# Attention scores in PSUM banks chosen by an account of expected times, and the narrower kind of scores first

## The chip, the cores and the metric

The kernel runs on one core of a Trainium2 chip. Its engines work from queues of their own: TensorE (PE in the profile, and PEld for its weight loads) multiplies matrices into PSUM; VectorE (DVE) and ScalarE (ACT) read PSUM; GpSimd (POOL) works in SBUF; SyncE (SP) issues most DMAs. A wait in a queue holds everything behind it in that queue. The metric is the device time of one execution in microseconds; the median of several runs counts.

## The reference, cut to what matters

Two layers over x of shape (2, 1024, 128), all in fp32: a retention block with group norm, latent attention (16 heads of 8, causal) with an expert choice behind it, plain attention (16 heads of 8) and a ternary-weight product, each followed by a residual sum and a layer norm. The change touches the two softmax attentions alone:

```
scores = jnp.einsum('bhqd,bhkd->bhqk', q, k) / np.sqrt(HEAD_DIM)     # first attention
causal = jnp.tril(jnp.ones((t, t), dtype=bool))
scores = jnp.where(causal, scores, -jnp.inf)
attn = jax.nn.softmax(scores, axis=-1)
out = jnp.einsum('bhqk,bhkd->bhqd', attn, v)
...
weights = jax.nn.softmax(scores, axis=-1)                            # second, not causal
out = jnp.einsum('bhqk,bhkd->bhqd', weights, v)
```

## The kernel before

The retention block takes the first 260 us. Then one long hand-ordered stretch (`tc.manual_schedule()`) runs both attentions as a chain of 224 items in ticks, with the other work of the layers (`side_work`: projections, experts, layer norms, outputs) put between the ticks. The order of instructions on every engine is the order of the Python calls.

**Steps and items.** A step is one attention (`a` = 0 causal, 1 plain), sequence `b`, block `k` of 512 queries and group `g` of four heads. The four heads of a group lie in the four row groups of 32 partitions, so that products of different heads can run in TensorE at once. Each step has *score items* (`s_items`: 128 queries against up to 512 keys) and, in the same number, *exponential items* (`t_items`: 128 keys against up to 512 queries). In the plain attention all of them have 512 columns; in the causal one they have 128, 256, 384 or 512.

**A tick** (`chain_tick`, L456) does, for the score item of this tick and the exponential item of 11 ticks earlier (`AHEAD`):
- first half: products `sc` of heads 0 and 1 (`score`), products `sct` of heads 2 and 3 (`shifted`), then DVE's row maxima of the two sc (`maxima`, L348 with the causal mask, L353 without) and ACT's exponentials of the two sct (`exps`, L397);
- second half: the same with heads 2 and 3 for sc, 0 and 1 for sct;
- where the causal diagonal needs it, a select on POOL (`bar`, L405);
- `product`: the exponentials of the item before, all four heads, times the values into one bank `acc`, which ACT copies out (L419, L422) and POOL adds up (L423);
- once a step: DVE joins the maxima (`shifts`), PE transposes them (`m_ps`, `enter`), and SP writes them into a row of q, so that sct comes out already lowered by the maximum; `finish` transposes the sums (`o_ps`) and DVE divides.

So a full tick writes nine PSUM tiles of one bank each: eight scores and acc. Side work takes more: `ph` and `pmoe` (the experts' products), `xn_ps`, `lpr`, `loT_ps` and others.

**Banks.** PSUM has eight banks in this kernel's pools. In this stretch every tile comes from `slot(name)`, which hands out the banks in a ring. A tile's first product waits until the last reader of the bank's previous tile is done; nothing else ties a bank to its user. In a full tick the ninth tile, acc, therefore gets the bank of the same tick's first sc, and every score tile gets a bank of the tick before.

Of the kernel before, what the change touches and what calls it, by code (L numbers as in the profile page):

```python
# [8 lines left out]
F32 = mybir.dt.float32  # L9
# [5 lines left out]
P = 128  # L15
B, T = 2, 1024
BT = 512
# [3 lines left out]
NG, GH, HD = 4, 4, 8  # L21
HW = 32
# [5 lines left out]
VW = HD + 1  # L28
VN = (NH - 1) * VW + HW
AHEAD = 11  # L30
# [30 lines left out]
def block_kernel(  # L61
# [19 lines left out]
    def mm(o, lhsT, rhs, start=True, stop=True):  # L81
        nc.tensor.matmul(o, lhsT, rhs, start=start, stop=stop)  # L82
# [64 lines left out]
    v_aug = [early.tile([P, T // P, VN], F32, name="v_aug_0")]  # L147
# [8 lines left out]
    banks, scratch_of = [None], [None]  # L156

    def slot(name):
        return banks[0](name)

    def ring_of(pools):
        turn = [0]

        def bank(name):

            at = turn[0] % 8
            turn[0] += 1
            return pools[at // 6].tile([P, BT], F32, tag=f"b{at}", name=name)

        return bank  # L170

    def hrows(j):
        return slice(j * HW, (j + 1) * HW)
# [140 lines left out]
    s_items, t_items = [], []  # L314
# [7 lines left out]
            t_items += [(i, kt, 0) for kt in range(T // P)]  # L322
    s_last = {it[0]: n for n, it in enumerate(s_items)}
    t_last = {it[0]: n for n, it in enumerate(t_items)}
    parts, lowered, es, sums, pools, o_tok = {}, {}, {}, {}, {}, []

    def score(item, heads):
        i, c, half, n = item
        a, b, k, g = steps[i]
        tok = slice(k * BT + c * P, k * BT + (c + 1) * P)  # L330
        if i not in parts:
            parts[i] = small.tile([P, NC, GH, NB], F32, tag="parts", name="parts")
        got = []
        for j in heads:
            sc = slot("sc")
            rws = hrows(j)
            mm(sc[:, :n], qT[b][rws, g, tok], kT[b][rws, g, half * BT : half * BT + n])
            got.append((j, sc))
        return got

    def maxima(item, got):
        i, c, half, n = item
        a, b, k, g = steps[i]
        for j, sc in got:
            part = parts[i][:, c, j, half : half + 1]
            if a == 0 and half == k:
                spare = early.tile([P, BT], F32, tag="spare", name="spare")
                nc.vector.tensor_tensor_reduce(  # L348
                    out=spare[:, :n], in0=sc[:, :n], in1=causal[:, BT - n :], scale=1.0,
                    scalar=-3.0e38, op0=ALU.add, op1=ALU.max, accum_out=part,  # L350
                )
            else:
                nc.vector.tensor_reduce(part, sc[:, :n], AX.X, ALU.max)  # L353

    def shifts(i):

        a, b, k, g = steps[i]
        n_half = NB if a else k + 1
        lowered[i] = small.tile([P, GH, NC], F32, tag="lowered", name="lowered")
        nc.vector.tensor_reduce(  # L360
            lowered[i].rearrange("p j c -> p c j"), parts[i][:, :, :, :n_half], AX.X, ALU.max,
            negate=True,
        )

    def enter(i):

        a, b, k, g = steps[i]
        tp = slot("m_ps")
        nc.tensor.transpose(
            tp[: GH * NC, :P], lowered[i].rearrange("p j c -> p (j c)"), ident  # L370
        )
        rows_of = small.tile([GH * NC, P], F32, tag="m_rows", name="m_rows", bufs=2)
        nc.scalar.copy(rows_of, tp[: GH * NC, :P])
        nc.sync.dma_start(out=qT[b][ONE::HW, g, block_of(k)], in_=rows_of)

    def shifted(n_item, heads):
        i, kt, lo = t_items[n_item]
        a, b, k, g = steps[i]
        n = BT - lo
        if n_item not in es:  # L380
            es[n_item] = pools["work"].tile([P, GH, BT], F32, tag="es", name="es")
        got = []
        for j in heads:
            sct = slot("sct")
            rws = hrows(j)
            mm(
                sct[:, :n], kT[b][rws, g, kt * P : (kt + 1) * P],
                qT[b][rws, g, k * BT + lo : (k + 1) * BT],
            )
            got.append((j, sct))  # L390
        return got

    def exps(n_item, got):
        i, kt, lo = t_items[n_item]
        n = BT - lo
        for j, sct in got:
            nc.scalar.activation(es[n_item][:, j, :n], sct[:, :n], AF.Exp, scale=scale)  # L397

    def bar(n_item):

        i, kt, lo = t_items[n_item]
        a, b, k, g = steps[i]
        if a == 0 and kt * P >= k * BT:
            d = es[n_item][:, :, :P]
            nc.gpsimd.affine_select(  # L405
                out=d, in_=d, pattern=[[0, GH], [1, P]], compare_op=ALU.is_ge, fill=0.0,
                base=0, channel_multiplier=-1,
            )

    def product(n_item):  # L410
        i, kt, lo = t_items[n_item]
        a, b, k, g = steps[i]
        acc = slot("acc")
        for j in range(GH):
            at = (g * GH + j) * VW
            mm(acc[hrows(j), lo:], v_aug[b][:, kt, at : at + HW], es[n_item][:, j, : BT - lo])
        if kt == 0:
            sums[i] = pools["work"].tile([P, BT], F32, tag="oT", name="oT")
            nc.scalar.copy(sums[i], acc)  # L419
        else:  # L420
            part = pools["work"].tile([P, BT], F32, tag="part", name="part", bufs=1)
            nc.scalar.copy(part[:, lo:], acc[:, lo:])  # L422
            nc.gpsimd.tensor_tensor(sums[i][:, lo:], sums[i][:, lo:], part[:, lo:], ALU.add)  # L423

    def finish(i):
        a, b, k, g = steps[i]
        tp = transposed(sums[i].rearrange("p (c t) -> p c t", c=NC), "o_ps")
        tp = tp.rearrange("p (h w) -> p h w", w=HW)
        rec = small.tile([P, NC * GH], F32, tag="rec", name="rec")
        nc.vector.reciprocal(rec, tp[:, :, ONE])  # L430
        nc.vector.tensor_tensor(
            o_tok[b][k][:, :, g * GH * HD : (g + 1) * GH * HD].rearrange(
                "p c (j d) -> p c j d", d=HD
            ),
            tp[:, :, :HD].rearrange("p (c j) d -> p c j d", c=NC),
            rec.rearrange("p (c j) -> p c j", c=NC).unsqueeze(3).to_broadcast([P, NC, GH, HD]),
            ALU.mult,
        )

    n_items = len(s_items)  # L440
# [15 lines left out]
    def chain_tick(tick):  # L456
        si = tick if tick < n_items else None
        ti = tick - AHEAD if 0 <= tick - AHEAD < n_items else None
        for s_heads, t_heads in (((0, 1), (2, 3)), ((2, 3), (0, 1))):
            got_s = score(s_items[si], s_heads) if si is not None else ()  # L460
            got_t = shifted(ti, t_heads) if ti is not None else ()
            if si is not None:
                maxima(s_items[si], got_s)
            if ti is not None:
                exps(ti, got_t)
        if ti is not None:
            bar(ti)
        if si is not None and s_last[s_items[si][0]] == si:
            shifts(s_items[si][0])
        ai = tick - AHEAD - 1  # L470
        if 0 <= ai < n_items:
            product(ai)
        si = tick - 1
        if 0 <= si < n_items and s_last[s_items[si][0]] == si:
            enter(s_items[si][0])
        ai = tick - AHEAD - 3
        if 0 <= ai < n_items and t_last[t_items[ai][0]] == ai:
            finish(t_items[ai][0])


    with ExitStack() as rc:
# [29 lines left out]
        at, n = R_CONST["cs"]  # L511
# [307 lines left out]
        with tc.manual_schedule():  # L819
# [46 lines left out]
            n = n_chunks - 1  # L866
# [11 lines left out]
        ring = []  # L878
        rp.close()
        ring.append(ctx.enter_context(  # L880
            tc.tile_pool(name="ring", bufs=1, space=PSUM, reuse_waits="tile")
        ))
        banks[0] = ring_of(ring)
        with tc.manual_schedule():
            chain_tick(0)
            normal(n, r)
            rs.close()
            ring.append(ctx.enter_context(tc.tile_pool(
                name="ring2", bufs=1, space=PSUM, side="right", reuse_waits="tile"
            )))  # L890
            aside(n, 1)
            chain_tick(1)
            pt, og = gated(n)
            affine(n, pt, og, range(RH))
            chain_tick(2)
            nc.vector.tensor_tensor(og, og, sg[n], ALU.mult)
            block = output(n, og)
            chain_tick(3)
            layer_norm(*block)
# [5 lines left out]
    for i, name in enumerate(("w1", "w2")):  # L905
        at, n = M_W[name]
# [179 lines left out]
    class Job:  # L1086
        def __init__(self, at, by, stages, after=()):
            self.at, self.by, self.stages, self.after, self.done = at, by, stages, after, False
# [177 lines left out]
```

## Time and profile before

| what | us |
|---|---|
| median of three runs | 1195.03 |
| lowest and highest | 1191.51, 1197.48 |
| the profiled execution, its time | 1191.54 |
| the profiled execution, its span | 1189.8 |
| mean granted TensorE clock in it | 0.975 |

The views are read as follows. A timeline line gives the start in us, the time in us to the end of a run of equal instructions, engine, source line, operation, out<-in, its shape and the number of instructions; in brackets the idle time before it and what ended that. A line L82 is the helper `mm` that records most products, so products are told apart by their tiles. An fp32 product stands as two matmul records, and a tick's length is read from the first `sc` of one tick to the first `sc` of the next.

Ticks begin at 264 us with tick 4. In the windows of the stretch, PE is busy 424.7 of the 452 us from 264 to 716 (the causal attention with most of the side work), 102.8 of the 104 us to 820 and 296.5 of the 316 us to 1136 (nearly all of the plain attention); DVE 313.4, 72.6 and 259.7; ACT 251.3, 65.2 and 239.5.

### The profile page before, as it was taken

The page shows a single profiled execution, that of the slowest core. Times are in us where ns is not written, and L with a number is a line of the kernel's source. Part 1 is how long each engine was busy: PE and PEld are TensorE (multiplying, and loading weights), DVE is VectorE, ACT ScalarE, POOL GpSimd, SP SyncE. Part 2 cuts the span into 40 slices and gives each one's busy share as a digit, 9 for nine tenths or more (in the row PEclk, how much of TensorE's full clock was granted, in tenths as well). Part 3 has the DMA queues.
Part 4 walks back from the last instruction along what each step waited for, and adds up shares of the span by engine and source line. Part 5 has one row for each costly group of instructions (what it writes and reads, how often), then busy time and mean ns, then how long its engine had stood idle before and what let it go on. Part 6 is the DMA issues. An engine that isn't in the chain of part 4 may idle for free.

```text
span 1189.8 us, 22189 instructions
## 1 busy us (share of the span) xinstructions
PE 1102.6 (93%) x8554; PEld 604.3 (51%) x8554; DVE 825.9 (69%) x1822; ACT 710.4 (60%) x1439; POOL 479.8 (40%) x491
## 2 busy tenths in 40 slices
PE   6999999979889999999999999999989989998993
PEld 5888888755444554554444444444333333333322
DVE  4666766757766667676666677667788888888812
ACT  2465544432666556655565557556768867886891
POOL 4466445411656434443353334423333333323342
PEclk9999999986999999999999999999999999999996
DMA  5511112101000000100010001000100000000000
GB/s 187 164 37 45 41 41 45 28 10 73 10 11 19 1 2 1 21 3 1 2 19 1 1 4 18 2 1 1 19 10 2 1 2 10 1 2 10 1 1 9
DMA packets 14840, 25.56 MB, mean 21 GB/s; under 512 B 2960, under 2 KB 8400, under 8 KB 14352
## 3 DMA queue, kind: packets, MB, share of 16 engines
q1 hardware_dynamic: 14080, 22.30, 7.7%
q8 instruction: 67, 1.10, 0.4%
q0 software_dynamic: 224, 1.05, 0.2%
q10 hardware_dynamic: 432, 0.81, 0.2%
q14 instruction: 37, 0.30, 0.1%
HBM read 10.13 MB, written 1.05 MB: 9 GB/s over the span
## 4 chain that ended last, share of the span: by engine, by line
PE 72%; DVE 17%; POOL 4%; issue 3%; ACT 2%; DMA 1%; SPq 0%; POOLq 0%; DVEq 0%; ACTq 0%
PE sc L82 17%; PE acc L82 15%; PE sct L82 12%; PE pmoe L82 5%; PE ph L82 5%; DVE parts L353 5%; DVE spare L348 2%; PE py L82 2%; PE pv L82 2%; PE pr L82 2%; PE pout L714 1%; PE o_ps L187 1%; PE pg L82 1%; DVE x L205 1%; ACT es L397 1%
## 5 line engine op out<-in xcount | busy, mean ns | idle before, releaser
L397 ACT ACTIVATE es<-sct 128x512 f32<-128x512 f32 (+3 forms) x896 | 426.9, 558 | 218.6 <-PE sct L82 169.0
L353 DVE TENSOR_REDUCE parts<-sc 128x1 f32<-128x512 f32 x640 | 396.9, 682 | 94.4 <-PE sct L82 69.0
L82 PE MATMUL sc<-kT,qT 32*128 32x512 f32 (+3 forms) x1792 | 428.4, 584 | 5.5 <-DVE parts L348 2.7
L82 PE MATMUL sct<-qT,kT 32*128 32x512 f32 (+3 forms) x1792 | 410.6, 578 | 1.4 <-DMA qT<-m_rows 1.1
L423 POOL TENSOR_TENSOR oT<-oT,part 128x512 f32<-128x512 f32 (+3 forms) x192 | 217.5, 1133 | 392.3 <-ACT part L422 388.0
L82 PE MATMUL acc<-es,v_aug 128*32 128x512 f32 (+3 forms) x1792 | 221.6, 558 | 40.6 <-DVE parts L353 29.0
L82 PEld LDWEIGHTS sc<-kT,qT 32*128 32x128 f32 x1792 | 171.7, 189 | 145.2 <-DVE parts L353 73.9
L82 PEld LDWEIGHTS sct<-qT,kT 32*128 32x128 f32 x1792 | 179.1, 184 | 46.0 <-issue 23.3
L348 DVE CUSTOM_DVE_ANT_0 spare<-sc,causal 128x512 f32<-128x512 f32 (+3 forms) x256 | 125.4, 490 | 48.2 <-PE sc L82 12.8
L82 PEld LDWEIGHTS acc<-es,v_aug 128*32 128x32 f32 x1792 | 37.8, 108 | 196.0 <-DVE parts L353 112.5
L422 ACT COPY part<-acc 128x512 f32<-128x512 f32 (+3 forms) x192 | 105.7, 550 | 42.4 <-PE acc L82 36.3
L405 POOL TENSOR_SCALAR_AFFINE_SELECT es<-es 128x512 f32<-128x512 f32 x64 | 40.8, 637 | 118.5 <-ACT es L397 118.5
L771 ACT ACTIVATE og<-pt,cols_sb 128x128 f32<-128x128 f32 x128 | 46.5, 468 | 53.1 <-PE pt L763 53.1
L82 PEld LDWEIGHTS pmoe<-m_w,hT 128*128 128x128 f32 x512 | 59.6, 192 | 16.2 <-DVE parts L353 8.8
L82 PE MATMUL pmoe<-m_w,hT 128*128 128x128 f32 x512 | 65.0, 280 | 0.6 <-DVE parts L348 0.2
L82 PE MATMUL ph<-xnT,m_w 128*128 128x512 f32 x128 | 62.4, 610 | 0.0
L118 POOL TENSOR_TENSOR rstd<-rstd,nhalf 128x4 f32<-128x4 f32 (+1 forms) x44 | 54.7, 1244 | 3.6
L970 DVE TENSOR_SCALAR hT<-ph,cols_sb 128x512 f32<-128x512 f32 x32 | 24.0, 750 | 35.2 <-PE ph L82 35.2
L645 POOL TENSOR_TENSOR swap<-swap,r_cs 128x1024 f32<-128x1024 f32 x16 | 38.7, 2417 | 20.7 <-DMA swap<-plain 20.7
L982 DVE SCALAR_TENSOR_TENSOR moe_acc<-pmoe,oh,moe_acc 128x128 f32<-128x128 f32 x64 | 22.4, 350 | 35.2 <-PE pmoe L82 34.8
L668 ACT COPY v<-pv 128x1024 f32<-128x1024 f32 x16 | 16.2, 1012 | 43.8 <-PE pv L82 43.8
L82 PEld LDWEIGHTS ph<-xnT,m_w 128*128 128x128 f32 x128 | 21.7, 189 | 31.0 <-issue 11.0
(178 smaller groups left out, 1190.1 us busy)
## 6 DMA issues: line engine op xcount, KB each, us to landing
swap<-plain SPq DMA_DIRECT2D x64, 128.0 KB
qT<-dense SPq DMA_DIRECT2D x32, 64.0 KB
kT<-dense SPq DMA_DIRECT2D x32, 64.0 KB
m_w<-in_m_w SPq DMA_DIRECT2D x2, 1024.0 KB
x<-in_x SPq DMA_DIRECT2D x4, 256.0 KB
mcs<-in_m_const SPq DMA_DIRECT2D x4, 256.0 KB
out<-ob SPq DMA_DIRECT2D x4, 256.0 KB
r_rest<-in_r_const POOLq DMA_DIRECT2D x1, 774.0 KB, 7.4
```

The lines of the kernel that those rows point to most:

```text
L82: nc.tensor.matmul(o, lhsT, rhs, start=start, stop=stop)
L118: nc.gpsimd.tensor_tensor(r, r, nhalf[:, :n], ALU.pow)
L348: nc.vector.tensor_tensor_reduce(out=spare[:, :n], in0=sc[:, :n], in1=causal[:, BT - n :], scale=1.0, scalar=-3.0e38, op0=ALU.add, op1=ALU ...
L353: nc.vector.tensor_reduce(part, sc[:, :n], AX.X, ALU.max)
L397: nc.scalar.activation(es[n_item][:, j, :n], sct[:, :n], AF.Exp, scale=scale)
L405: nc.gpsimd.affine_select(out=d, in_=d, pattern=[[0, GH], [1, P]], compare_op=ALU.is_ge, fill=0.0, base=0, channel_multiplier=-1,)
L422: nc.scalar.copy(part[:, lo:], acc[:, lo:])
L423: nc.gpsimd.tensor_tensor(sums[i][:, lo:], sums[i][:, lo:], part[:, lo:], ALU.add)
L645: nc.gpsimd.tensor_tensor(swap[n], swap[n], table(n, 1), ALU.mult)
L771: nc.scalar.activation(og[:, a, g, :], pt[a][:, g, :], AF.Identity, bias=col("gn_b", h), scale=col("gn_w", h))
L970: nc.vector.tensor_scalar(hT[:, f, :], ph, bias, 0.0, ALU.add, ALU.max)
L982: nc.vector.scalar_tensor_tensor(acc[:, c, :], py[:, :P], oh[:, c, e : e + 1], acc[:, c, :], ALU.mult, ALU.add)
```

## The change

The ring is replaced by a class, `Banks`. It keeps, while the program is being written, an account of its own: a time for PE, one for each row group, one for DVE and one for ACT, and for each bank the time at which it is expected free. `take` gives the bank with the earliest such time among those not held. A score tile is held from its `take` until its maximum or exponential has been written; `settle` drops what is held at the start of a tick. Tiles of side work (through `slot`) get a bank in the same way, with fixed costs. The account's numbers: a product of n columns keeps its row group n/1180 us; a maximum takes 0.06 + n/960 us and starts 0.2 us after its product, a masked one 0.31 + n/960; an exponential or a copy takes 0.27 + n/1900 and starts 0.25 us after. Nothing of the account is executed on the chip: it only chooses banks.

Second, within each half of a tick the two `sct` products are issued ahead of the two `sc` products where they have fewer columns. The maxima are still written ahead of the exponentials.

```diff
-    def ring_of(pools):
-        turn = [0]
-        def bank(name):
-            at = turn[0] % 8
-            turn[0] += 1
-            return pools[at // 6].tile([P, BT], F32, tag=f"b{at}", name=name)
-        return bank
+    class Banks:
+        def __init__(self, pools):
+            self.pools, self.free, self.held = pools, [0.0] * 8, []
+            self.pe, self.rows, self.vec, self.sca = 0.0, [0.0] * 4, 0.0, 0.0
+        def take(self, name):
+            known = [b for b in range(6 if len(self.pools) == 1 else 8) if b not in self.held]
+            bank = min(known, key=lambda b: self.free[b])
+            self.held.append(bank)
+            return bank, self.pools[bank // 6].tile([P, BT], F32, tag=f"b{bank}", name=name)
+        def __call__(self, name):
+            bank, t = self.take(name)
+            self.pe = max(self.pe, max(self.rows), self.free[bank]) + 0.9
+            self.vec, self.sca = max(self.vec, self.pe) + 0.3, max(self.sca, self.pe) + 0.3
+            self.free[bank] = self.pe + 1.2
+            return t
+        def settle(self):
+            self.held = []
+        def rows_product(self, bank, j, n):
+            self.pe = max(self.pe, self.rows[j], self.free[bank])
+            self.rows[j] = self.pe + n / 1180.0
+            return self.rows[j]
+        def all_rows_product(self, bank, n, ready):
+            self.pe = max(self.pe, max(self.rows), self.free[bank], ready) + 0.3 + n / 1180.0
+            self.rows = [self.pe + 0.1] * 4
+            return self.pe
+        def on_vector(self, bank, at, us):
+            self.vec = self.free[bank] = max(self.vec, at + 0.2) + us
+            self.held.remove(bank)
+        def on_scalar(self, bank, at, us):
+            self.sca = self.free[bank] = max(self.sca, at + 0.25) + us
+            self.held.remove(bank)
+            return self.sca
...
-            sc = slot("sc")
+            bank, sc = banks[0].take("sc")
...
-            got.append((j, sc))
+            got.append((j, sc, bank, banks[0].rows_product(bank, j, n)))
...
+                banks[0].on_vector(bank, at, 0.31 + n / 960.0)
...
+                banks[0].on_vector(bank, at, 0.06 + n / 960.0)
...
+            ready_at[n_item] = banks[0].on_scalar(bank, at, 0.27 + n / 1900.0)
...
-        acc = slot("acc")
+        bank, acc = banks[0].take("acc")
+        at = banks[0].all_rows_product(bank, BT - lo, ready_at[n_item])
...
+        banks[0].on_scalar(bank, at, 0.27 + (BT - lo) / 1900.0)
...
+        banks[0].settle()
         for s_heads, t_heads in (((0, 1), (2, 3)), ((2, 3), (0, 1))):
+            short_t = si is not None and ti is not None and BT - t_items[ti][2] < s_items[si][3]
+            got_t = shifted(ti, t_heads) if short_t else ()
             got_s = score(s_items[si], s_heads) if si is not None else ()
-            got_t = shifted(ti, t_heads) if ti is not None else ()
+            if ti is not None and not short_t:
+                got_t = shifted(ti, t_heads)
...
-        banks[0] = ring_of(ring)
+        banks[0] = Banks(ring)
```

`shifted` takes its banks as `score` does, and the remaining edits pass the bank and the account's time along.

More of the change, by code (lines that the diff above doesn't have):

```diff
@@ L324, in block_kernel @@
     t_last = {it[0]: n for n, it in enumerate(t_items)}
-    parts, lowered, es, sums, pools, o_tok = {}, {}, {}, {}, {}, []
+    parts, lowered, es, ready_at, sums, pools, o_tok = {}, {}, {}, {}, {}, {}, []
     def score(item, heads):
@@ L343, in maxima @@
         a, b, k, g = steps[i]
-        for j, sc in got:
+        for j, sc, bank, at in got:
             part = parts[i][:, c, j, half : half + 1]
@@ L383, in shifted @@
         for j in heads:
-            sct = slot("sct")
+            bank, sct = banks[0].take("sct")
             rws = hrows(j)
@@ L389, in shifted @@
             )
-            got.append((j, sct))
+            got.append((j, sct, bank, banks[0].rows_product(bank, j, n)))
         return got
@@ L395, in exps @@
         n = BT - lo
-        for j, sct in got:
+        for j, sct, bank, at in got:
             nc.scalar.activation(es[n_item][:, j, :n], sct[:, :n], AF.Exp, scale=scale)
+            ready_at[n_item] = banks[0].on_scalar(bank, at, 0.27 + n / 1900.0)
     def bar(n_item):
@@ L412, in product @@
         a, b, k, g = steps[i]
-        acc = slot("acc")
+        bank, acc = banks[0].take("acc")
+        at = banks[0].all_rows_product(bank, BT - lo, ready_at[n_item])
         for j in range(GH):
-            at = (g * GH + j) * VW
-            mm(acc[hrows(j), lo:], v_aug[b][:, kt, at : at + HW], es[n_item][:, j, : BT - lo])
+            first = (g * GH + j) * VW
+            mm(acc[hrows(j), lo:], v_aug[b][:, kt, first : first + HW], es[n_item][:, j, : BT - lo])
         if kt == 0:
@@ L469, in chain_tick @@
             shifts(s_items[si][0])
-        ai = tick - AHEAD - 1
-        if 0 <= ai < n_items:
+        ai = tick - AHEAD - 1 if 0 <= tick - AHEAD - 1 < n_items else None
+        if ai is not None:
             product(ai)
@@ L475, in chain_tick @@
             enter(s_items[si][0])
-        ai = tick - AHEAD - 3
-        if 0 <= ai < n_items and t_last[t_items[ai][0]] == ai:
+        ai = tick - AHEAD - 3 if 0 <= tick - AHEAD - 3 < n_items else None
+        if ai is not None and t_last[t_items[ai][0]] == ai:
             finish(t_items[ai][0])
```

## The prediction

> **What bounds the kernel now.** First the page's busy shares and its chain of waits:
>
> ```profile
> PE 1102.6 (93%) x8554; PEld 604.3 (51%) x8554; DVE 825.9 (69%) x1822; ACT 710.4 (60%) x1439; POOL 479.8 (40%) x491
> ...
> PE 72%; DVE 17%; POOL 4%; issue 3%; ACT 2%; DMA 1%; SPq 0%; POOLq 0%; DVEq 0%; ACTq 0%
> ```
>
> PE (TensorE) is busy in 93% of the span and carries 72% of the chain; DVE (VectorE) carries 17%. So the question is what a tick costs on PE. Second view: the timeline of PE in one all-512 tick without side work, which begins at T = 903.80.
>
> ```profile
> 903.80 0.70 PE L82 MATMUL sc<-kT,qT 32*128 32x512 f32 x2
> 903.82 0.70 PE L82 MATMUL sct<-qT,kT 32*128 32x512 f32 x2
> 904.34 0.59 PE L82 MATMUL sc<-kT,qT 32*128 32x512 f32 x2
> 904.35 1.01 PE L82 MATMUL sct<-qT,kT 32*128 32x512 f32 x4
> 904.78 0.59 PE L82 MATMUL sc<-kT,qT 32*128 32x512 f32 x2
> 905.20 0.59 PE L82 MATMUL sct<-qT,kT 32*128 32x512 f32 x2
> 905.21 0.59 PE L82 MATMUL sc<-kT,qT 32*128 32x512 f32 x2
> 905.73 1.07 PE L82 MATMUL acc<-es,v_aug 128*32 128x512 f32 x8
> 906.73 0.70 PE L82 MATMUL sc<-kT,qT 32*128 32x512 f32 x2
> ```
>
> Each product runs in two passes (8 records for 4 products). A first pass takes 0.53 us (903.80 to 904.34), a second 0.43 (904.34 to 904.77, within the x4 row). The first half-tick starts at T, the second at T+0.97, acc at T+1.93, the next tick at T+2.93. Third, what empties the banks, from the timelines of DVE and of ACT (ScalarE) in the same tick:
>
> ```profile
> 904.96 1.29 DVE L353 TENSOR_REDUCE parts<-sc 128x1 f32<-128x512 f32 x2 [0.60 <-PE sct L82]
> ```
> ```profile
> 904.00 0.59 ACT L422 COPY part<-acc 128x512 f32<-128x512 f32 x1
> 905.05 1.08 ACT L397 ACTIVATE es<-sct 128x512 f32<-128x512 f32 x2 [0.46 <-PE sct L82]
> ```
>
> The first maximum starts at T+1.16 and takes 0.68 (the mean of its group, 682 ns), so the first sc bank comes free at T+1.84. The previous tick's acc bank is free at T+0.79 (904.59). Before the tick's work DVE idles 0.60 and ACT 0.46: PE alone sets the length of this tick. In the ring its last sct, due at T+0.97, takes that acc bank and waits for nothing.
>
> **The change, part by part.** *Instructions.* The built orders of DVE, ACT, POOL and SP are the same, DMAs included; PE has the same instructions, 384 of them swapped within 48 ticks. So nothing is added or removed but bank waits, and I listed for each tile of both built orders whose end its bank waits for. In the ring the only tile that waits for work of its own tick is acc, for the first maximum (T+1.84, hidden: acc is due at T+1.93). In the changed order 116 ticks have a score tile of the second half-tick on a bank of the first: 54 all-512 ticks (the last or last two sct wait for the first sc's maximum) and 62 causal ones (mostly the last sc, waiting for the first sct's exponential, ACT).
>
> *Why the account picks them.* It prices a product of 512 columns at 512/1180 = 0.43 us; the trace shows two passes. It thus thinks the first sc bank free at 0.43+0.2+0.59 = T+1.23 (measured T+1.84), its tick shorter than ACT's four exponentials and copy at 0.54 each, and the acc bank late: followed through the code for this sort of tick it expects that one at about T+1.5 (measured T+0.79).
>
> *Price in an all-512 tick.* What a late pair costs is shown by a tick of before at 480, whose second half waits for a maximum:
>
> ```profile
> 481.15 0.37 PE L82 MATMUL sc<-kT,qT 32*128 32x128 f32 x1
> 481.17 0.70 PE L82 MATMUL sct<-qT,kT 32*128 32x512 f32 x2
> ...
> 482.22 0.32 PE L82 MATMUL acc<-es,v_aug 128*32 128x128 f32 x4
> ```
>
> From a late start to acc it is 1.05 us. The sct, whose bank was long free, went 0.02 us after the sc that waited ahead of it: a waiting product holds all that follows on PE's queue, here the rest of the half-tick, acc, and behind it ACT's copy and POOL's add (which have slack: POOL is idle 60%). With 0.06 us from release to start (the maximum before ended at 481.09) the changed tick is 1.84+0.06 = T+1.90 for the last sct, +1.05 = T+2.95 for acc, +1.00 = 3.95 us against 2.93. If nothing were late it would cost 0; if the late sct's loads were also exposed, 0.19 more (a weight load). I take 3.95, the nearest row.
>
> *Sum, all-512 ticks.* From tick 148 on (878.6 us) 49 of 76 ticks carry it. 39 are plain, now 3.04 us on average: 39 x 0.915 = 35.7, and 7 of these also transpose m_ps, 0.2 each: +37.1. Eight have an o_ps transpose (0.59; now 3.61 on average): 4.55, +7.5. Two more (now 5.06) and five earlier ones at +0.9: +6.3. Together +51; bounds +35 (0.7 a tick, if the longer tick hides more) and +62.
>
> *Causal ticks.* An sc of 512 with an sct of 384, the tick at T = 570.25:
>
> ```profile
> 570.26 0.92 PE L82 MATMUL sct<-qT,kT 32*128 32x384 f32 x4
> ...
> 571.53 0.49 PE L82 MATMUL sct<-qT,kT 32*128 32x384 f32 x2
> 572.25 0.64 PE L82 MATMUL acc<-es,v_aug 128*32 128x512 f32 x4 [0.21 <-DVE parts L353]
> ```
>
> The sct ends at T+0.93, but its exponential began only at 571.49, after the sc had ended too (571.37): ACT waits for a count of PE's products in program order. With the shorter kind first I let it begin at T+0.95; it takes 0.49 (mean of the 384 form) and frees the bank at T+1.44, so the last sc starts at 1.50 and acc at 2.55 instead of 2.00: +0.55, or +0.84 if the count doesn't help. Ten such ticks, two of them with a maximum in place of the exponential (+0.75): +5.9. With an sct of 256: 0.71 end, 0.39 exponential, acc at 2.24: 7 x 0.24 = 1.7. With 128: acc at 1.91, nothing; 9 ticks at 0. The short sc ones (128 or 256 against an sct of 512): the release moves 0.3 us later than that which the same sct waits for now, 16 x 0.3 = 4.8. The other 12 at 0.3: 3.6. Together +16, and +2 for the eight ticks at the start, where PE waits for inputs anyway. Bounds -5 (the earlier exponentials pay) and +35.
>
> *What is saved.* Ticks without a wait of this sort start with all banks drained: 15 plain all-512 ticks of 3.18 on average fall to 2.93, -3.7. In the stretches with the outputs job, where DVE's layer norms make the maxima late and ticks take 4.15 to 4.37, acc gets an ACT bank instead of the first maximum's; but DVE is busy there nearly without a gap (870.2 to 879.3), so I take -3 (bounds 0 and -10). Causal ticks without the wait: -6 (0 and -12). Sum: 51+16+2-3.7-3-6 = +56 on the profiled execution's 1191.5 us (span 1189.8): 1247.5. The median of the runs lay 3.5 higher (1195.0); I say 1249.
>
> *Order within a tick.* The second half now issues the sct on rows 0 to 63 before the sc on rows 64 to 127 where sct is shorter. In before an sct starts ahead of an sc that was issued ahead of it, when its rows are free first:
>
> ```profile
> 360.74 1.22 PE L82 MATMUL sct<-qT,kT 32*128 32x512 f32 x5
> 361.39 0.28 PE L82 MATMUL sc<-kT,qT 32*128 32x128 f32 x2
> ```
>
> So the order costs nothing by itself; its cover is that rows run independently. The Trainium skill, "TensorE: Matmul & The Clock Gate", section "Step-by-step: what each phase is for", says that matmuls stay in program order and only weight loads are pulled ahead. This trace contradicts it across row groups by 0.65 us. By the page the late half's sc would start at T+0.97 and acc at T+2.02 in place of 1.91 in the nine ticks with an sct of 128, +1 us; by the row, 0.
>
> **Rivals.** *R1, the account pays: faster.* Banks are spread away from late maxima. For it: in the view of waits the weight loads of acc stand idle 112.5 us behind DVE's maxima, and twelve ticks of 4.15 to 4.37 exceed 2.93 by 1.2 to 1.4. If acc ran 1 us earlier in these twelve and the causal ticks gave 12, with the in-tick waits at 0.08 us each (+9), it is -12-12+9 = -15: 1180. It decides if a wait costs under 0.2 us on average (24 over 116); against it, T+1.84 can't move, being a product's end plus one maximum. *R2, a smaller loss.* Waits at 0.7 (+35), causal ticks even (0), savings at their bound (-20): 1210. Against it: PE has no slack in the plain tick. *R3, nothing.* The picks equal the ring's in effect: 1195. The listed waits speak against. *R4, a larger loss.* The pauses, up to 0.5 us in 54 ticks, lower the granted clock, which stood at 0.83 in the 200 to 300 us stretch (PE waits there) and 1.00 after: if 10% of the 260 us from tick 148 to the last scores ran at half, +26: 1275.
>
> **How the numbers follow.** Forecast 0.66 (own range 1225 to 1270), R2 0.18, R1 0.08, R3 0.04, R4 0.04. The predicted time is the forecast's. From 1212 to 1272 lies the forecast but for a tenth of it and most of R2: 0.8. About 0.5% can be told from no change here (three runs span 6 us): faster 0.08, same 0.04, slower 0.88.
>
> **What would show it.** In the changed profile plain all-512 ticks near 900 us of about 3.95, with the last sct starting alone at T+1.90 right after the first maximum, and DVE idle about 1.5 us a tick in place of 0.6; PE's idle before sct naming DVE parts; the ticks with ph or pmoe products from 756 to 815 unchanged at 4.84 to 5.0 (5.3 with o_ps); the 512/384 ticks near 570 longer by 0.5. It is wrong if the last sct starts at T+0.97, or if an all-512 step of eight ticks still takes 25.2 us (903.80 to 929.00).

## The result, and the profile after

| kernel | median us (lowest to highest) | ratio to before, 95% interval |
|---|---|---|
| before | 1193.59 (1191.51 to 1197.48, 4 runs) | |
| changed | 1246.95 (1244.92 to 1247.64, 4 runs) | 1.0437 [1.0417, 1.0456] |

The change costs 53.4 us. The profiled execution of the changed kernel took 1244.92 us with a span of 1243.2, also 53.4 more than the span before. Its page has the same two lines that were read of before:

```profile
PE 1186.8 (95%) x8554; PEld 619.8 (50%) x8554; DVE 818.8 (66%) x1822; ACT 721.7 (58%) x1439; POOL 478.9 (39%) x491
...
PE 79%; DVE 11%; POOL 4%; ACT 2%; issue 2%; DMA 1%; SPq 0%; POOLq 0%; DVEq 0%; ACTq 0%
```

The instructions are as many as before, and yet PE is busy 84.2 us longer (1102.6 before), its share is higher, and the chain of waits blames DVE less, not more. Read alone, this page says that PE has more to do. The timeline says what really happens. PE in a plain all-512 tick of the changed kernel, which starts at T = 923.07:

```profile
923.07 0.70 PE L82 MATMUL sc<-kT,qT 32*128 32x512 f32 x2
923.09 0.70 PE L82 MATMUL sct<-qT,kT 32*128 32x512 f32 x2
923.61 0.59 PE L82 MATMUL sc<-kT,qT 32*128 32x512 f32 x2
923.62 1.00 PE L82 MATMUL sct<-qT,kT 32*128 32x512 f32 x3
924.05 0.59 PE L82 MATMUL sc<-kT,qT 32*128 32x512 f32 x2
924.47 0.59 PE L82 MATMUL sct<-qT,kT 32*128 32x512 f32 x1
924.48 0.59 PE L82 MATMUL sc<-kT,qT 32*128 32x512 f32 x2
924.98 1.12 PE L82 MATMUL sct<-qT,kT 32*128 32x512 f32 x2
926.03 1.06 PE L82 MATMUL acc<-es,v_aug 128*32 128x512 f32 x8
927.03 0.70 PE L82 MATMUL sc<-kT,qT 32*128 32x512 f32 x2
```

The two passes of the last sct run from 924.98 (T+1.91) to 926.10, from 925.07 on by themselves, while three of the four row groups do nothing; acc follows at T+2.96, and the next tick begins at T+3.96 (2.93 in the tick shown of before). The weight loads and DVE of the same tick name the cause:

```profile
924.98 0.29 PEld L82 LDWEIGHTS sct<-qT,kT 32*128 32x128 f32 x2 [0.73 <-DVE parts L392]
```
```profile
924.23 2.48 DVE L392 TENSOR_REDUCE parts<-sc 128x1 f32<-128x512 f32 x4 [1.47 <-PE sct L82]
```

The first maximum starts at 924.23, takes 0.68 and so ends at 924.91; the sct's weights are loaded 0.07 after that. DVE in turn idles 1.47 us a tick in place of 0.60. The sct waits for a maximum that began 0.03 us after its own product had ended (923.61 + 0.59 = 924.20), so it could hardly be earlier; and the profile files the time under "PE busy", since one row group is running for most of it.

The ticks add up as follows, each measured from its first score product, of either kind, to that of the next:

| ticks | number | before us | changed us | difference |
|---|---|---|---|---|
| all-512, from tick 148, a second-half tile on a first-half bank | 49 | 157.4 | 203.7 | +46.3 |
| the same, ticks 113 to 147 | 5 | 19.8 | 25.5 | +5.6 |
| causal (19 to 112), with such a tile | 54 | 231.9 | 244.0 | +12.1 |
| causal, without | 40 | 177.2 | 173.3 | -3.9 |
| first ticks (4 to 18) | 15 | 49.6 | 52.4 | +2.8 |
| plain all-512, from tick 148, without | 15 | 47.7 | 43.9 | -3.8 |
| with the outputs job, from tick 148 | 12 | 52.2 | 48.5 | -3.7 |
| other all-512, 113 to 147 | 30 | 135.6 | 133.2 | -2.4 |

Together +53.0 of the 53.4 us; the ten ticks at the end without sc are the same.

In the causal tick that was shown of before (there at 570.25, here T = 579.70) the views of ACT and then of PE read

```profile
580.64 1.74 ACT L437 ACTIVATE es<-sct 128x384 f32<-128x384 f32 x4 [2.13 <-PE sct L82]
```
```profile
581.18 1.12 PE L82 MATMUL sc<-kT,qT 32*128 32x512 f32 x2
582.24 0.64 PE L82 MATMUL acc<-es,v_aug 128*32 128x512 f32 x4
```

The exponentials do begin earlier (T+0.94, before T+1.24), and in spite of it the last sc waits for the first of them until T+1.48 and acc for the sc until T+2.54, 0.54 later than before.

### The profile page after: what moved, and what is told of

The parts are those of the page before. It is cut to its first block, busy times and chain, and to the rows that moved or that the text cites. A ratio compares the mean times of both kernels' runs of the same rounds, so it can differ in the third digit from the quotient of the medians.

```text
span 1243.2 us, 22182 instructions
## 1 busy us (share of the span) xinstructions
PE 1186.8 (95%) x8554; PEld 619.8 (50%) x8554; DVE 818.8 (66%) x1822; ACT 721.7 (58%) x1439; POOL 478.9 (39%) x491
## 4 chain that ended last, share of the span: by engine, by line
PE 79%; DVE 11%; POOL 4%; ACT 2%; issue 2%; DMA 1%; SPq 0%; POOLq 0%; DVEq 0%; ACTq 0%
PE sc L82 19%; PE sct L82 18%; PE acc L82 14%; PE pmoe L82 5%; PE ph L82 5%; DVE parts L392 3%; PE py L82 2%; PE pv L82 2%; PE pr L82 2%; PE o_ps L225 1%; PE pout L762 1%; ACT es L437 1%; PE pg L82 1%; PE psc L82 1%; PE pt L811 1%
## 5 line engine op out<-in xcount | busy, mean ns | idle before, releaser
L437 ACT ACTIVATE es<-sct 128x512 f32<-128x512 f32 (+3 forms) x896 | 435.5, 557 | 230.9 <-PE sct L82 228.9
L82 PE MATMUL sct<-qT,kT 32*128 32x512 f32 (+3 forms) x1792 | 463.1, 581 | 3.2 <-DVE parts L392 1.4
L82 PE MATMUL sc<-kT,qT 32*128 32x512 f32 (+3 forms) x1792 | 444.4, 592 | 3.8 <-DVE on L796 2.5
L82 PEld LDWEIGHTS sc<-kT,qT 32*128 32x128 f32 x1792 | 177.7, 190 | 129.3 <-DVE parts L392 32.5
L82 PEld LDWEIGHTS sct<-qT,kT 32*128 32x128 f32 x1792 | 175.4, 185 | 116.1 <-DVE parts L392 41.4
L82 PEld LDWEIGHTS acc<-es,v_aug 128*32 128x32 f32 x1792 | 36.9, 108 | 178.4 <-ACT es L437 84.2
L82 PE MATMUL py<-r_wo,og 128*128 128x128 f32 x256 | 34.4, 292 | 3.4 <-DVE og L895 2.0
```

## The experiments

The theory: the whole loss comes of score tiles that the account puts into a bank of their own tick, and it does so because it prices a product at half its time. The rivals: the new order within a tick; many small shifts of banks in place of this one wait; a fixed price for any broken half-tick.

**The account alone.** The bank account of the change, the order of before:

```diff
-            short_t = si is not None and ti is not None and BT - t_items[ti][2] < s_items[si][3]
+            short_t = False
```

> The account chooses the banks, the order of the two kinds of scores is that of before. All 54 all-512 ticks keep a second-half sct on a bank of the first half, and the causal ones have 63 such picks. Theory (the waits inside a tick cost the time): within 10 us of the changed kernel, 1237 to 1257 us. Rival (the new order costs it): near the kernel before, 1190 to 1200 us.

Measured: 1255.37 us (1253.82 to 1256.56), ratio 1.0505 [1.0477, 1.0533]. The account alone brings all of the loss; the order isn't its cause and takes 8 us of it back. The 49 late all-512 ticks again take 203.7 us. The 8 us lie mostly in the first 15 ticks (62.8 us against 52.4 with the new order); why there is open. Here 117 ticks have such a tile, 116 in the changed kernel (119 and 118 tiles).

**The order alone.** The ring of before, with the five lines of the change in `chain_tick` that put the narrower kind first:

```diff
-            got_t = shifted(ti, t_heads) if ti is not None else ()
+            if ti is not None and not short_t:
+                got_t = shifted(ti, t_heads)
```

> The ring chooses the banks, the narrower kind goes first in 48 causal ticks. No score tile waits for work of its own tick. Theory: not slower than before; acc, which takes the bank of the tick's first tile, gets one that ScalarE empties early instead of the first maximum's, so up to 0.3 us less in each of 48 ticks: 1178 to 1194 us. Rival (the order holds up the later products of a half-tick): 1200 to 1250 us.

Measured: 1195.3 us (1191.62 to 1200.32, ten runs), ratio 1.001 [0.9989, 1.003]: no change. The rival falls, but the gain that I expected isn't there either. Its mechanism is: in the tick shown above of before and of the changed kernel (here T = 575.34) the timelines of ACT and PE have

```profile
576.28 1.36 ACT L397 ACTIVATE es<-sct 128x384 f32<-128x384 f32 x3 [1.77 <-PE sct L82]
```
```profile
577.05 0.64 PE L82 MATMUL acc<-es,v_aug 128*32 128x512 f32 x4
```

that is, exponentials at T+0.94 and acc at T+1.71 in place of T+1.24 and T+2.00. The 23 ticks with sc of 512 and sct of 384 or 256 gain 3.4 us, but the 19 with other mixes of a narrower sct lose 2.6, and the first ticks 0.8: it cancels.

**No bank of the first half for the second half.** A bank stays held until all eight score tiles of the tick are placed; the account's prices stay as wrong as they are:

```diff
         def on_vector(self, bank, at, us):
             self.vec = self.free[bank] = max(self.vec, at + 0.2) + us
-            self.held.remove(bank)
...
             self.sca = self.free[bank] = max(self.sca, at + 0.25) + us
-            self.held.remove(bank)
...
+        banks[0].settle()
         if ti is not None:
             bar(ti)
```

> The changed kernel, but no bank of a tick's first half goes to its second half: a bank is held until the tick's scores are all placed. Everything else of the account stays, its wrong prices too. Theory: the 118 waits inside ticks are the whole loss, and the plain all-512 ticks near 900 us go back to 2.93 to 3.1: 1178 to 1200 us. Rival (the account's other choices cost too): over 1215 us.

Measured: 1179.11 us (1178.22 to 1180.15), ratio 0.9872 [0.9849, 0.9894], 67.8 us below the changed kernel and 15.7 below the ring. The 49 late ticks take 157.3 us (157.4 before). What comes back is 14 us more than the change had cost: the waits inside a tick are the whole loss, and the other choices of the account gain against the ring, in the outputs ticks (48.5 us for 52.2) as elsewhere.

**The price of one such wait, in the ring.** The ring, in which the last sct and acc swap banks in 76 ticks:

```diff
+    swap_at = [0]
...
-            at = turn[0] % 8
+            at = (turn[0] + swap_at[0]) % 8
...
         for j in heads:
+            swap_at[0] = 1 if j == 1 and 148 <= n_item + AHEAD < n_items else 0
             sct = slot("sct")
+            swap_at[0] = 0
...
+        swap_at[0] = -1 if 148 <= n_item + AHEAD + 1 < n_items else 0
         acc = slot("acc")
+        swap_at[0] = 0
```

> The ring of before, with one swap of banks in each of the 76 all-512 ticks from tick 148 on: the last sct takes the bank of the tick's first sc, and acc the one that the last sct had. Theory: the price of one such wait is 0.9 to 1.0 us in a tick that is not otherwise held up, less in the 12 ticks with late layer norms: 55 to 75 us more than before, 1249 to 1269 us. Rival (the loss comes of many small shifts, not of this one wait): under 1215 us.

Measured: 1263.6 us (1258.97 to 1263.97), ratio 1.057 [1.0541, 1.0599], 68.8 us more than before. The 76 ticks grew by 67.8 us; the 49 which the change also hits by 46.4, the same as there (46.3) although no other tile changed its bank. Plain ticks take 3.95 us; in one (T = 910.66) the PE timeline reads

```profile
912.56 1.12 PE L82 MATMUL sct<-qT,kT 32*128 32x512 f32 x2
913.61 1.07 PE L82 MATMUL acc<-es,v_aug 128*32 128x512 f32 x8
914.61 0.70 PE L82 MATMUL sc<-kT,qT 32*128 32x512 f32 x2
```

that is, the last sct at T+1.90, acc at T+2.95 and the next tick at T+3.95, as in the changed kernel. One wait explains the tick.

**The same wait, one maximum later.** As above, with the second sc's bank in place of the first's:

```diff
-            swap_at[0] = 1 if j == 1 and 148 <= n_item + AHEAD < n_items else 0
+            swap_at[0] = 2 if j == 1 and 148 <= n_item + AHEAD < n_items else 0
...
-        swap_at[0] = -1 if 148 <= n_item + AHEAD + 1 < n_items else 0
         acc = slot("acc")
-        swap_at[0] = 0
```

> The ring with the last sct of the 76 late all-512 ticks on the bank of the tick's second sc, which comes free one maximum (0.60 us) after the first. Theory (the tick's length follows the release: release + 0.06 + 1.05 + 1.00): 0.6 us a tick more than with the first sc's bank (1263.6 us), about 46 us in all, 1295 to 1320 us. Rival (a broken half-tick costs a fixed restart, whatever it waits for): 1258 to 1275 us.

Measured: 1308.33 us (1304.41 to 1310.48), ratio 1.094 [1.0917, 1.0963]. PE in a plain tick of this kernel (T = 911.81):

```profile
913.22 0.59 PE L82 MATMUL sc<-kT,qT 32*128 32x512 f32 x2
914.31 1.12 PE L82 MATMUL sct<-qT,kT 32*128 32x512 f32 x2 [0.50 <-DVE parts L355]
915.36 1.07 PE L82 MATMUL acc<-es,v_aug 128*32 128x512 f32 x8
916.36 0.70 PE L82 MATMUL sc<-kT,qT 32*128 32x512 f32 x2
```

The sct starts at T+2.50, 0.60 later than in the swap before this, and the tick lasts 4.55 us, 0.60 more; in all it is 44.7 us more than with the first sc's bank. The length follows the release; a fixed restart is ruled out. Only here, where the other products of the half-tick have ended long before, does PE show an idle time before the sct.

**The account with the traced prices.** Two passes a product, and the pitch and latency of maxima and exponentials as in the trace of before:

```diff
-            self.rows[j] = self.pe + n / 1180.0
+            self.rows[j] = self.pe + 0.1 + n / 590.0
...
-            self.pe = max(self.pe, max(self.rows), self.free[bank], ready) + 0.3 + n / 1180.0
-            self.rows = [self.pe + 0.1] * 4
+            self.pe = max(self.pe, max(self.rows), self.free[bank], ready) + 0.12 + n / 590.0
+            self.rows = [self.pe] * 4
...
-            self.vec = self.free[bank] = max(self.vec, at + 0.2) + us
+            self.vec = max(self.vec, at + 0.2) + us
+            self.free[bank] = self.vec + 0.08
...
-            self.sca = self.free[bank] = max(self.sca, at + 0.25) + us
+            self.sca = max(self.sca, at + 0.25) + us
+            self.free[bank] = self.sca + 0.1
...
-            ready_at[n_item] = banks[0].on_scalar(bank, at, 0.27 + n / 1900.0)
+            ready_at[n_item] = banks[0].on_scalar(bank, at, 0.23 + n / 1940.0)
```

> The changed kernel with the account's prices taken from the trace of before: a score product keeps its rows 0.1 + n/590 us (two passes), acc 0.12 + n/590, an exponential 0.23 + n/1940 with 0.1 us until its bank is free, a maximum 0.08 us until its bank is free. It makes no pick inside a tick in the all-512 ticks and 27 in causal ones; acc takes the first sct's bank in all of the late ticks. Theory (the wrong price of a product made the picks): 1172 to 1190 us. Rival (an account can't beat the ring, since side work isn't in it): 1195 us or more.

Measured: 1177.42 us (1175.88 to 1182.69), ratio 0.9861 [0.9834, 0.9888]. With the traced prices alone, and no rule about halves, the picks inside all-512 ticks are gone and so is the loss. But these are several prices at once, of products and of their readers. Followed through its code, the account with the score product's price alone put right picks no such bank in any all-512 tick (42 ticks in the causal ones are left). With the product's price left as it was and only the readers' put right, it picks none there either (64 in the causal ones). So the halved price of a product makes these picks only together with the rough prices of the readers, and no run tells the two apart. That side work is priced roughly doesn't keep the account from beating the ring.

**Both: traced prices and banks held.** The edits of the last kernel and of the third together.

> Both: the account with the traced prices, and banks held until the tick's scores are placed, so no picks inside a tick at all. Theory: the 27 remaining waits of the account with traced prices cost 0.2 to 0.5 us each, so 5 to 12 us less than that kernel, 1165 to 1180 us, and the fastest of all. Rival (those waits are hidden): the same time as that kernel within 2 us.

Measured: 1175.53 us (1173.34 to 1176.69), ratio 0.9831 [0.9816, 0.9845], 20 us below the ring and 71 below the changed kernel. It is the lowest median, but its range overlaps that of the last kernel, and I had expected 5 to 12 us between them: the medians differ by 1.9, which is what the rival said. The 27 waits cost less than I said, though not nothing: from tick 19 on the ticks that have them differ by 3.9 us in all (the other ticks give 2.4 of it back), most of it in the ones with a short sc (up to 1.0 us each); where the last sc waits for an exponential of 128 columns it costs nothing.

**Banks held, order of before.** The third kernel with `short_t = False`.

> Banks held for the tick under the change's own prices, with the order of before (sc always first). Against the same with the narrower kind first (1179.1 us) it tells what the order is worth when no wait lies inside a tick. Theory (the order matters through the banks' waits alone, since rows start independently): within 5 us, 1174 to 1185 us. Rival (the order itself gains by earlier exponentials): over 1187 us.

Measured: 1181.38 us (1179.6 to 1181.89), ratio 0.9879 [0.9864, 0.9894], 2.3 us more than with the narrower kind first. The two were taken on different chips, and beside the kernel before, as run with each, they are at 0.9879 and 0.9872, so the order is worth some 1 to 2 us here, which is within the intervals.

## Why the prediction was right, point by point

I said 1249 us with 1212 to 1272 around it, as slower by 56 us on the profiled execution; it was 53.4. (The sum gives 1247.5 from the profiled execution and 1251 from the median; 1249 lies between them.) The mechanism held, and the parts were off by 4 us at most; that the sum came out within 3 us is partly luck, as the errors of the parts partly cancel.

- *One wait inside the tick, T+1.90 for the last sct, T+2.95 for acc, 3.95 us a tick.* Measured T+1.91, T+2.96 and 3.96. Shown by the swap in the ring, which makes the same tick with this one wait, and by the later release, which moves it by just 0.60.
- *+46.4 from the 49 late ticks* (37.1+7.5+1.8): +46.3. *+4.5 from the five earlier ones:* +5.6, since in tick 136 the sct also waited behind DVE's layer norms (5.27 to 7.05).
- *Causal ticks with such a wait, +16:* +12.1. By parts, sct of 384 +5.9 said, +4.2 measured (eight of the ten at 0.53 to 0.94, one at 0.01 and one at -0.50); of 256 +1.7, +1.6; of 128 nothing, -0.8 for nine; the short sc ones +4.8, +5.6; the other 12, for which I had taken a flat 0.3 each, +3.6, +1.5. This last was the most mis-sized.
- *First ticks +2:* +2.8. *Savings of -3.7, -3 and -6:* -3.8, -3.7 and -3.9, and -2.4 in ticks 113 to 147, which I hadn't counted.
- *Why the account picks these banks.* That a wrong price makes the picks was argued from the code, and the kernel with traced prices shows it of the prices together. That it is the product's alone isn't shown: by the code the readers' prices had to be wrong too.
- *The order costs nothing by itself.* Shown by the order alone (ratio 1.001) and with held banks (1 to 2 us the other way). The nine ticks with an sct of 128 tell it from the rule of the Trainium skill ("TensorE: Matmul & The Clock Gate", section "Step-by-step: what each phase is for") that matmuls stay in program order. The lines at 360.74 and 361.39 of before contradict it already, and in one of these nine ticks of the changed kernel (T = 590.08) the PE timeline has

```profile
590.40 1.22 PE L82 MATMUL sc<-kT,qT 32*128 32x512 f32 x5
591.05 0.39 PE L82 MATMUL sct<-qT,kT 32*128 32x128 f32 x4
591.98 0.64 PE L82 MATMUL acc<-es,v_aug 128*32 128x256 f32 x8
```

  At 590.40 a sc of the second half begins, 0.65 us ahead of the two sct that were issued before it, and acc starts at T+1.90: as by the row (1.91), not as by the page (2.02).
- *Signs.* DVE idles 1.47 us in such a tick (1.5 said), the ticks from 756 to 815 us stayed at 4.84 to 4.96 (5.33 with o_ps), and the 512/384 ticks grew by 0.54. One sign failed: I expected PE's own idle time to name the maxima. In the plain ticks it shows on PE's weight loads alone, since another row group keeps PE "busy".
- *Rivals.* R1 was wrong of the whole, but its mechanism is there: of the outputs ticks two between 142 and 147 fell from 4.21 to 3.21, as acc no longer waits for a late maximum. R2 and R3 fell with the 49 late ticks, which pay the full price (+51.9 with the five earlier ones, not +35 or nothing). R1 decides once the waits inside the tick are gone, and then gives 14 to 20 us. R4 fell: the granted clock was 0.970 against 0.975 on the whole and 1.00, 0.99 and 1.00 in the windows from 728 us to 835, to 1000 and to 1189. In these, the clock stood at half for a single stretch of 3.4 us, so the pauses cost about 1.7 us by it at most.

## What to carry to other kernels

Before a planner's choices are trusted, put its prices beside one traced tick: with a product counted at half its time, and its readers priced roughly, it saw a bank free 0.6 us early and another 0.7 us late, and the waits that came of it cost 53 us. With buffers few and a stage that fills and empties them, a reuse inside the stage puts fill, drain and refill end to end, while a reuse across stages is hidden; a rule that forbids the first was worth about as much as prices taken from the trace (1179.1 and 1177.4 us). And a wait in one of several row groups need not show as idle time: compare the length of the same tick, not the busy share.

## What the runs showed of the hardware that was not expected

PE's busy time rose by 84.2 us (1102.6 to 1186.8) with the same instructions and 53.4 us more span, so the busy time counts a lone product of 32 rows like four of them at once: in the late tick at 923.07 PE stands as busy for all of the 3.96 us. And ACT's first exponential in a tick waits for the products issued ahead of its own too: in the same causal tick (512 and 384 columns) it began at T+1.24 in all five kernels that issue sc first, though its own product had ended by T+0.93, and at T+0.94 to 0.95 in all five that issue sct first.
